# A decoder layer with sixteen experts: eight buffers for target rows, one softmax moved to the second expert, one power moved ahead of four sends

## The chip, the core and the metric

The kernel runs on one core of a Trainium2 chip. A core has four engines for computing: TensorE (PE in the profile; PEld is its loading of weights), VectorE (DVE), ScalarE (ACT) and GpSimd (POOL). SyncE (SP) issues transfers, as do ScalarE and GpSimd. Each engine works through its own list of instructions strictly in order and waits where an instruction's inputs or its buffer are not ready. The metric is the device time of one execution in microseconds (us); the median of the runs is compared.

## What is computed

One decoder layer on 1,024 tokens (16 sequences of 64) of 256 features in fp32: self-attention of 16 heads, cross-attention on a compressed context, and a feed-forward layer with a shared expert and 16 routed experts, each after a layernorm without weights. Only the last part matters here:

```python
scores = softmax(xt @ Wg.T)                    # 16 experts
sg = scores.reshape(T, 4, 4)                   # four groups
gmask = two best groups by their maximum
topi = top_k(where(gmask, sg, -inf), 4)        # four experts for a token
weights = take_along_axis(scores, topi)
h = silu(xt @ W1[e].T) * (xt @ W3[e].T)        # each expert e
y = sum over the chosen e of weights * (h @ W2[e].T)
z = (silu(xt @ Ws1.T) * (xt @ Ws3.T)) @ Ws2.T  # shared expert
x = x + y + z
```

The choice needs only the order of the logits, so the kernel takes it from the logits, and computes the softmax, which gives the weights, apart.

## The kernel before

The tokens lie in eight tiles of 128, in two halves of four tiles. Matrices that need more precision than one pass gives are split into a rounded part and a rest: ScalarE casts the rounded part (`parts_of`, L111; line L112 in the profile) and VectorE subtracts it from the source (L113).

**Towards the experts.** The third layernorm of the second half (`layernorm_t(3, (1,), ...)`, L1183) computes mean and variance on VectorE (L165 to L169), the variance to the power of -1/2 on GpSimd (`rstd`, L172), and a shift on VectorE (L176); ScalarE and VectorE scale the rows (L194, L187), TensorE turns them (L208). Then `choose(1)` (L1185) finds each token's four experts and, for each choice, the row in a DRAM array `xd` where the token goes (`targets`, L818). `send` (L821) writes rows by indirect DMAs, which GpSimd issues (L826), four for each choice of a half. The order on GpSimd around the change was: two choices of the first half (eight sends), choice 2 of the first half (four sends, L1197, not before the shared expert's last subtraction), the power `rstd` of the second half, choice 3 of the first half (L1200), and all four choices of the second half (sixteen sends, L1201).

**The routed experts.** Fifteen experts (e0 to e14) work on 384 slots each; the sixteenth is computed densely. The loop at L1336 runs in stages: its turn e loads the inputs of expert e, computes the hidden layer of expert e-1 and the output of expert e-2.

- `expert_inputs` (L1234): SP loads the expert's slots from `xd` into `xr` (three buffers; a load waits for the sends of the choices that can reach it). TensorE turns them, ScalarE and VectorE split them into `xs`. VectorE then copies one column, which says where each row of the output goes, as integers into `to` (L1253). `to` has four buffers.
- `expert_weights` (L1223, `weight_parts` at L268): SP loads 640 KB into a raw tile (two buffers), ScalarE casts them (L270), VectorE and, from the fourth expert on, also GpSimd subtract (L275).
- `expert_hidden` (L1256): 18 matmuls of 384 columns, silu on ScalarE (L1266, L1269), products on VectorE (L1267, L1270), the split into `hp`.
- `send_outputs` (L1274): 15 matmuls into two PSUM tiles, which two copies on ScalarE and one on VectorE evict into `y` (L1282; two buffers), and three indirect DMAs on GpSimd (L1287), which send the rows of `y` to where `to` says. `to` and `y` come free when these transfers have landed.

**The weights of the choices.** `weights_of_choices(half)` (L853) computes the softmax over 16 logits and picks each choice's weight: 14 short instructions on VectorE (L859 to L881, with `choices`, L726, among them) and an exp on ScalarE (L862). ScalarE holds the tables of either exp or silu, so a table is loaded ahead of the exp and another ahead of the next silu. The first half's call is at L1175; the second half's at L1360, in turn 6 of the loop. The results are read after the loop, when `add_outputs` (L1310) adds the experts' outputs, and by `add_last` (L934).

A planner puts the instructions of each engine in order, by a modelled timeline; `tc.issue_after(ins)` keeps what is written under it from being issued before `ins`.

Of the kernel before, what the change touches and what calls it, by code (L numbers as in the profile page):

```python
# [27 lines left out]
U32 = mybir.dt.uint32  # L28
# [15 lines left out]
SLOTS = 384  # L44
# [27 lines left out]
def decoder_layer(ctx: ExitStack, tc: tile.TileContext, a: dict, out: bass.AP):  # L72
# [79 lines left out]
    variances, rstds, shifts, highs, lows = [], [], [], [], []  # L152
    norms, scaled, turned, silus, exps, softened = [], [], [], [], [], []
# [153 lines left out]
    with ExitStack() as attn:  # L307
# [513 lines left out]
        def send(half, choices=range(TOPK), waits=()):  # L821

            to = targets[half]
            for k in choices:
                for i in range(4):
                    sent = nc.gpsimd.indirect_dma_start(  # L826
                        out=xd[: TOPK * NT + (E - 1 - k) * SLOTS],
                        out_offset=bass.IndirectOffsetOnAxis(ap=to[:, k, i : i + 1], axis=0),
                        in_=rows[half][i // 2][:, i % 2, :],
                        in_offset=None,  # L830
                    ).ins
                    side_by_side(sent, sent_rows)
                    sent_for[k].append(sent)
                    behind(sent, waits)
# [18 lines left out]
        def weights_of_choices(half):  # L853


            shape = [128, 4, E]
            lg = logits[half]
            m = fs.tile([128, 4], F32, tag="r_m", name="r_m")
            nc.vector.tensor_reduce(m, lg, AX.X, ALU.max)  # L859
            p = fs.tile(shape, F32, tag=f"r_p{half}", name=f"r_p{half}")  # L860
            nc.vector.tensor_tensor(p, lg, m.unsqueeze(2).broadcast_to(shape), ALU.subtract)
            exps.append(nc.scalar.activation(p, p, AF.Exp).ins)  # L862
            s = fs.tile([128, 4], F32, tag="r_s", name="r_s")
            nc.vector.tensor_reduce(s, p, AX.X, ALU.add)
            nc.vector.reciprocal(s, s)
            nc.vector.tensor_tensor(p, p, s.unsqueeze(2).broadcast_to(shape), ALU.mult)
            sel = selected[half]
            last = fs.tile([128, 4], F32, tag=f"cl{half}", name=f"cl{half}")
            nc.vector.tensor_tensor(last, sel[:, :, E - 1], p[:, :, E - 1], ALU.mult)
            nth = fs.tile(shape, F32, tag="slot", name="nth_back")  # L870
            nc.vector.tensor_tensor(
                nth, places[half], sel[:, :, E - 1 :].broadcast_to(shape), ALU.add
            )
            ch = choices(nth, sel)
            kept = fs.tile(shape, F32, tag="slot", name="kept")
            nc.vector.scalar_tensor_tensor(kept, over[half], 0.5, p, ALU.is_lt, ALU.mult)
            nc.vector.tensor_tensor(
                ch, ch, kept.unsqueeze(1).broadcast_to([128, TOPK, 4, E]), ALU.mult
            )
            w = fs.tile([128, TOPK, 4], F32, tag=f"cw{half}", name=f"cw{half}")  # L880
            nc.vector.tensor_reduce(w, ch, AX.X, ALU.add)  # L881
            return w, last, p
# [57 lines left out]
        routed = []  # L940


        with (
# [169 lines left out]
            for n in range(len(units) + 2):  # L1113
# [62 lines left out]
                if n == 9:  # L1176
                    rows[1] = [
                        xw.tile([128, 3, 2, 2, DC], F32, tag="w_s", name="rows1")
                        .rearrange("p a b c d -> p (a b c d)")[:, : 2 * ROW]
                        .rearrange("p (a b) -> p a b", a=2)  # L1180
                        for _ in range(2)
                    ]
                    normed[1] = layernorm_t(3, (1,), token_rows(1))[0]  # L1183
                    high = highs[-1]
                    scored, placed, aimed = choose(1)  # L1185
                    sh = [
                        xb.tile([128, 2, 2, 4 * HQ], F32R, tag=f"w_q{m}", name=f"sh{m}")
                        .rearrange("p a b c -> p (a b c)")
                        for m in range(2)
                    ]  # L1190
                    hs = []
                    for k in range(3):
                        with after(*pn_turned[(0 if k else 1) :]):
                            up = shared_up(0, k, xa)
                            part = [t[:, k * 512 : (k + 1) * 512] for t in sh]
                            hs.append(shared_hidden(k, *up, xa, part))
                    send(0, (2,), [lows[-1]])  # L1197
                    with after(projected, scaled[-1]):
                        shared_output(0, hs)
                    send(0, (3,), [high])  # L1200
                    send(1)  # L1201
                    with after(high):
                        dense_ups = dense_up(0, turned[-1], scored, scored)
                    with after(aimed, scored):
                        ups = [shared_up(1, 0, xa)]
                    with after(aimed, placed):
                        ups.append(shared_up(1, 1, xa))
                        hs = [shared_hidden(k, *ups[k], xa) for k in range(2)]
                        ups.append(shared_up(1, 2, xa))
                        hs.append(shared_hidden(2, *ups[2], xa))  # L1210
                        h_p = dense_gated(*dense_ups)
                        shared_output(1, hs)
                        dense_out(h_p, 0, range(4), add_last)
# [3 lines left out]
    fx = ctx.enter_context(tc.tile_pool(name="fx", bufs=2, reuse_waits="tile"))  # L1217
# [5 lines left out]
    def expert_weights(src, down_lo=nc.gpsimd):  # L1223
        return weight_parts(
            src,
            fw.tile([128, W_COLS], F32, tag="w123", name="w123"),
            [
                fw.tile([128, W_COLS], F32R, tag=f"w123{n}", name=f"w123{n}", bufs=3)
                for n in range(2)
            ],  # L1230
            down_lo,
        )

    def expert_inputs(e):  # L1234

        t = fx.tile([128, SLOTS // 128, ROW], F32, tag="xr", name="xr", bufs=3)
        first = TOPK * NT + (E - 2 - e) * SLOTS
        load = nc.sync.dma_start(
            out=t, in_=xd[first : first + SLOTS].rearrange("(b p) d -> p b d", p=128)
        ).ins  # L1240
        for k in range(min(TOPK, e + 1)):
            behind(load, sent_for[k])
        to = fx.tile([128, SLOTS // 128], U32, tag="to", name="to", bufs=4)
        parts = [fx.tile([128, 2, SLOTS], F32R, tag=f"xs{n}", name=f"xs{n}") for n in range(2)]
        for c in range(2):
            ps = at_tile([128, 512])[:, :SLOTS]
            for b in range(SLOTS // 128):
                nc.tensor.transpose(
                    ps[:, b * 128 : (b + 1) * 128], t[:, b, c * 128 : (c + 1) * 128], ident
                )  # L1250
            lows.append(parts_of(ps, parts[0][:, c, :], parts[1][:, c, :]))
        with tc.issue_after(lows[-1]):
            nc.vector.tensor_copy(to, t[:, :, D + e])  # L1253
        return parts, to
# [81 lines left out]
    for e in range(E + 1):  # L1336
        if e in (1, 2):

            low = lows[-1]
            hs[e - 1] = expert_hidden(ws[e - 1], xs[e - 1][0], SLOTS)  # L1340
        if e < E - 1:
            low = lows[-1]
            with tc.issue_after(up_done[0] if e in (1, 2) else low):
                xs[e] = expert_inputs(e)
            if e >= 1:
                with tc.issue_after(low), tc.issue_after(silus[-1]):
                    ws[e] = expert_weights(a["W123"][e], nc.vector if e < 3 else nc.gpsimd)
        if 0 <= e - 1 < E - 1 and e > 2:
            hs[e - 1] = expert_hidden(ws[e - 1], xs[e - 1][0], SLOTS)
        if e - 2 >= 0:  # L1350
            if e == E:

                with tc.issue_after(gated[0]):
                    h_p = dense_hidden(w_last, 1, 0)
            last = send_outputs(e - 2, ws.pop(e - 2), hs.pop(e - 2), xs.pop(e - 2)[1])
            if e - 2 == E - TOPK - 2:
                short = slots_are_short()
            if e == 6:
                with tc.issue_after(gated[0]), tc.issue_after(silus[-1]):
                    routed.append(weights_of_choices(1))  # L1360
            k = e - 2 - (E - 1 - TOPK)
            if k >= 0:
                got[k] = load_outputs(k)
# [135 lines left out]
```

## Time and profile before

| | |
|---|---|
| runs | 593.65, 597.68, 601.36 us (median 597.68) |
| the profiled execution | 590.21 us, of which the span is 588.4 |
| granted TensorE clock, mean | 0.979 of full speed |
| busy, share of the span | PE 92%, PEld 76%, DVE 68%, ACT 47%, POOL 39% |
| indirect output sends (L1287) | 45, mean 1084 ns on GpSimd, 2.4 to 7.1 us to landing |
| expert weights (`w<-in_W`) | 15 loads of 640 KB, median 4.7 us to landing |
| power on GpSimd (L172) | 1062 ns |
| table load on ScalarE | 1.28 us |

Times are microseconds from the span's start. In the page's slices a digit is a tenth of busy time. In the timeline each line gives start, length, engine, source line, operation, output and inputs, and in brackets how long the engine stood idle before it and whose end released it; "issue" there means that the profile shows nothing it waited for. Releasers are inferred, so an engine named as releaser may stand for a transfer that ended just then.

### The profile page before, as it was taken

The page shows a single profiled execution, that of the slowest core. Times are in us where ns is not written, and L with a number is a line of the kernel's source. Part 1 is how long each engine was busy: PE and PEld are TensorE (multiplying, and loading weights), DVE is VectorE, ACT ScalarE, POOL GpSimd, SP SyncE. Part 2 cuts the span into 40 slices and gives each one's busy share as a digit, 9 for nine tenths or more (in the row PEclk, how much of TensorE's full clock was granted, in tenths as well). Part 3 has the DMA queues.
Part 4 walks back from the last instruction along what each step waited for, and adds up shares of the span by engine and source line. Part 5 has one row for each costly group of instructions (what it writes and reads, how often), then busy time and mean ns, then how long its engine had stood idle before and what let it go on. Part 6 is the DMA issues. An engine that isn't in the chain of part 4 may idle for free.

```text
span 588.4 us, 10571 instructions
## 1 busy us (share of the span) xinstructions
PE 540.4 (92%) x3999; PEld 444.3 (76%) x3999; DVE 401.0 (68%) x879; ACT 279.4 (47%) x524; POOL 230.1 (39%) x213
## 2 busy tenths in 40 slices
PE   5979999999999999999999999999989778889962
PEld 4868988989889885667777577685778678879861
DVE  5434546475365788868476586889758667889876
ACT  3655575575745522231432323252625366857551
POOL 4192010010000104534343444632554646768762
PEclk9988999999999999999999999999999999999995
DMA  8667041240400398673020000000512676666384
GB/s 241 168 194 212 17 144 64 80 137 23 130 1 1 89 293 244 171 214 91 1 60 11 8 1 1 0 29 1 184 65 67 220 234 225 219 215 219 107 274 158
DMA packets 56293, 70.82 MB, mean 120 GB/s; under 512 B 13872, under 2 KB 42768, under 8 KB 56240
## 3 DMA queue, kind: packets, MB, share of 16 engines
q1 hardware_dynamic: 51408, 58.71, 33.6%
q0 software_dynamic: 3696, 10.36, 4.6%
q10 hardware_dynamic: 1136, 1.05, 0.5%
q8 instruction: 32, 0.52, 0.4%
q14 instruction: 21, 0.17, 0.1%
HBM read 48.61 MB, written 21.86 MB: 120 GB/s over the span
## 4 chain that ended last, share of the span: by engine, by line
PE 71%; DVE 12%; DMA 6%; ACT 4%; issue 4%; POOL 2%; SPq 0%; DVEq 0%; ACTq 0%; POOLq 0%
PE mm L104 42%; PE mm L989 6%; PE av L583 5%; PE at L566 4%; DMA yd<-y,to 4%; PE at L335 3%; PE at L1012 2%; PE av L1025 2%; PE av L104 2%; PE mm L431 2%; ACT w L270 2%; DVE rt L968 1%; DVE w L275 1%; DMA w<-in_W 1%; DVE x L1317 1%
## 5 line engine op out<-in xcount | busy, mean ns | idle before, releaser
L974 POOL TENSOR_TENSOR roped<-rt,rt 128x512 f32<-128x512 f32 x48 | 62.6, 1327 | 82.8 <-DVE rt L968 80.5
L968 DVE TENSOR_TENSOR rt<-mm,rope_q 128x512 f32<-128x512 f32 x96 | 61.5, 684 | 23.7 <-PE mm L104 23.0
L104 PE MATMUL mm<-xn,w_q 128*128 128x512 f32 x288 | 74.1, 403 | 0.5 <-ACT xn L214 0.5
L104 PEld LDWEIGHTS mm<-xn,w_q 128*128 128x128 f32 x288 | 52.1, 188 | 14.3 <-issue 2.6
L104 PE MATMUL mm<-xs,w 128*128 128x384 f32 x270 | 54.5, 344 | 8.3 <-ACT w L270 3.2
L1287 POOL DMA_INDIRECT yd<-y,to x45 | 48.8, 1084 | 26.0 <-ACT y L1282 7.5
L104 PEld LDWEIGHTS mm<-xs,w 128*128 128x128 f32 x270 | 45.8, 188 | 11.5 <-ACT w L270 4.2
L319 ACT ACTIVATE p<-p 128x512 f32<-128x512 f32 x32 | 20.2, 630 | 67.2 <-DVE p L318 67.2
L514 POOL TENSOR_TENSOR wo<-code,scale 128x512 fp32r<-128x512 f32 x8 | 10.6, 1328 | 103.2 <-PE mm L104 94.4
L989 PE MATMUL mm<-roped,w_s 128*64 128x512 f32 x192 | 46.3, 601 | 0.0
L606 DVE TENSOR_TENSOR x<-mm,x 128x256 f32<-128x256 f32 x64 | 26.0, 419 | 28.6 <-PE mm L104 27.4
L104 PE MATMUL mm<-wo,o 128*128 128x256 f32 x256 | 39.6, 295 | 0.1
L104 PE MATMUL mm<-wv,xn 128*128 128x256 f32 x256 | 37.0, 297 | 2.4 <-ACT kT L551 2.4
L104 PE MATMUL av<-w,hp 128*128 128x256 f32 x225 | 35.1, 289 | 4.0 <-DVE y L1282 3.3
L316 DVE TENSOR_REDUCE sm_m<-at 128x8 f32<-128x512 f32 x32 | 21.7, 680 | 22.8 <-PE at L566 21.9
L104 PEld LDWEIGHTS mm<-wv,xn 128*128 128x128 f32 x256 | 33.4, 197 | 3.5 <-ACT kT L551 2.6
L104 PE MATMUL mm<-xn,wk 128*128 128x512 f32 x128 | 35.6, 409 | 0.0
L104 PE MATMUL mm<-xn,wq 128*128 128x512 f32 x128 | 34.7, 407 | 0.4 <-ACT xn L214 0.4
L104 PEld LDWEIGHTS av<-w,hp 128*128 128x128 f32 x225 | 30.5, 188 | 5.7 <-DVE y L1282 3.9
L583 PE MATMUL av<-pt,v 128*128 128x128 f32 x256 | 34.5, 277 | 0.0
L104 PEld LDWEIGHTS mm<-wo,o 128*128 128x128 f32 x256 | 32.9, 190 | 1.5 <-issue 0.4
L583 PEld LDWEIGHTS av<-pt,v 128*128 128x128 f32 x256 | 32.0, 191 | 1.2
(216 smaller groups left out, 1138.8 us busy)
## 6 DMA issues: line engine op xcount, KB each, us to landing
w<-in_W SPq DMA_DIRECT2D x15, 640.0 KB, 4.7
code<-in_codes SPq DMA_DIRECT2D x32, 256.0 KB, 3.3
scale<-in_scales SPq DMA_DIRECT2D x32, 256.0 KB, 4.8
xr<-xd SPq DMA_DIRECT2D x15, 408.0 KB, 4.8
xd<-zeros SPq DMA_DIRECT2D x8, 720.0 KB, 7.0
yd<-zeros SPq DMA_DIRECT2D x8, 512.0 KB, 6.9
got<-yd SPq DMA_DIRECT2D x16, 256.0 KB, 4.3
wq<-in_Wq SPq DMA_DIRECT2D x4, 512.0 KB, 3.5
```

The costliest lines, as they stand in the source:

```text
L104: m = nc.tensor.matmul(ps, lhsT=l, rhs=r, start=(n == 0), stop=(n == len(pairs) - 1))
L270: nc.scalar.copy(w[0], t)
L316: nc.vector.tensor_reduce(m, sc, AX.X, ALU.max)
L319: exps.append(nc.scalar.activation(p, p, AF.Exp, scale=scale).ins)
L335: last = nc.tensor.transpose(ps[:, 2 * n : 2 * n + 2, :].rearrange("p a q -> p (a q)"), pn[:, 2 * n : 2 * n + 2, :].rearrange("p a k -> p ...
L566: nc.tensor.matmul(sc[par * 64 : par * 64 + 64, 2 * g + pp, :], lhsT=qk[0][:, b * S : (b + 1) * S], rhs=qk[1][:, b * S : (b + 1) * S], sta ...
L583: nc.tensor.matmul(av[:, k * 128 : (k + 1) * 128], lhsT=v[:, i, k0 : k0 + HD], rhs=pt[:, i].rearrange("p a q -> p (a q)"), start=True, sto ...
L606: nc.vector.tensor_tensor(x[i], ps, x[i], ALU.add)
L968: nc.vector.tensor_tensor(mt, ps3, rope_table(t, 2 * ab + k), ALU.mult)
L974: nc.gpsimd.tensor_tensor(r.rearrange("p (b s) -> p b s", s=S), one, two, op)
L989: nc.tensor.matmul(ps[h // 2][(h % 2) * 64 : (h % 2) * 64 + 64], lhsT=w_s[:, t, blk, ab, :], rhs=roped[2 * t + ab], start=first[h], stop=l ...
L1287: sent = nc.gpsimd.indirect_dma_start(out=yd[: (E - 1) * SLOTS + min(TOPK, E - 1 - e) * NT], out_offset=bass.IndirectOffsetOnAxis(ap=to[:, ...
```

## The change

Three edits, independent of each other in the text of the program:

```diff
-                    send(0, (2,), [lows[-1]])
+                    with tc.issue_after(rstds[-1]):
+                        send(0, (2,), [lows[-1]])
...
-        to = fx.tile([128, SLOTS // 128], U32, tag="to", name="to", bufs=4)
+        to = fx.tile([128, SLOTS // 128], U32, tag="to", name="to", bufs=8)
...
+        if e == 1:
+            with tc.issue_after(gated[0]), tc.issue_after(silus[-1]):
+                routed.append(weights_of_choices(1))
         if 0 <= e - 1 < E - 1 and e > 2:
...
-            if e == 6:
-                with tc.issue_after(gated[0]), tc.issue_after(silus[-1]):
-                    routed.append(weights_of_choices(1))
```

The first keeps the four sends of choice 2 behind the power of the third layernorm's second half, so that the power comes ahead of them on GpSimd. The second gives the target rows `to` eight buffers in place of four, 12 bytes a partition each. The third takes the second half's softmax from turn 6 of the loop to turn 1, after expert 0's last product has been split. In the planned order the softmax then stands on VectorE between the splits of e0 and e1's products, and its exp on ScalarE ahead of e1's silu. From e8 on the planner also sets some neighbouring instructions differently: on ScalarE the weight cast of some experts comes behind a silu and a cast that it came before, of others ahead of them, and on GpSimd three sends of e5 stand together ahead of a subtraction that stood between them.

## The prediction

> **What bounds the kernel now.** I first read the page's forty slices of 14.7 us. The columns are equal slices of the span, the digits tenths of busy time.
>
> ```profile
> PE   5979999999999999999999999999989778889962
> ...
> DMA  8667041240400398673020000000512676666384
> ```
>
> TensorE is full almost everywhere until slice 31; from there to slice 38 (about 456 to 557 us) it falls to 7 and 8 while the DMA engines stand at 5 to 7. That is the loop over fifteen routed experts (e0 to e14), and all three edits act there or just ahead of it. I split it into stretches: TensorE was busy 30.4 of 33 us (424 to 457), 24.1 of 33 (457 to 490), 13.9 of 14.5 (490 to 504.5), 21.8 of 26 (504.5 to 530.5), 23.2 of 25 (530.5 to 555.5). So the loop is bound by TensorE in good stretches and by something else in two bad ones. The timeline says by what; columns: start, length, engine, instruction, and in brackets the idle time before it and who ended it. Ahead of the loop:
>
> ```profile
> 431.70 0.96 POOL L826 DMA_INDIRECT xd<-wkq,to  x1 [0.30 <-issue]
> 432.69 1.06 POOL L172 TENSOR_TENSOR ln_rstd<-ln_var,half_power 128x4 f32<-128x4 f32 x1
> 433.78 0.16 DVE L176 SCALAR_TENSOR_TENSOR ln_shift<-ln_mv,ln_rstd 128x4 f32<-128x4 f32 x1 [3.94 <-POOL ln_rstd L172]
> ...
> 434.63 1.15 PE L208 MATMUL av<-ident,rows 128*128 128x128 f32 x8 [2.37 <-ACT rows L194]
> ```
>
> The variance was ready at 429.84, but the power stood behind four sends; VectorE waited 3.94 us, TensorE 2.37. At e3 and e4:
>
> ```profile
> 479.04 1.26 ACT L270 CAST w<-w 128x1280 fp32r<-128x1280 f32 x1 [4.77 <-DMA w<-in_W]
> ...
> 482.59 0.98 POOL L1287 DMA_INDIRECT yd<-y,to  x1 [0.16 <-DVE to L1253]
> ...
> 488.91 0.17 DVE L1253 CAST to<-xr 128x3 uint32<-128x3 f32 x1 [3.13 <-DMA yd<-y,to]
> ...
> 489.96 0.86 PE L104 MATMUL av<-w,hp 128*128 128x256 f32 x5 [2.46 <-DVE y L1282]
> ```
>
> e3's weights come late, since their load is queued on SP behind row loads that wait for the last send. e0's third output send then leaves at 482.59 and lands at 488.7; e4's target copy needs that buffer, and the eviction that TensorE wants stands behind the copy. At e6 to e9:
>
> ```profile
> 505.21 1.28 ACT L862 ACT_TABLE_LOAD   x1
> ...
> 506.78 1.28 ACT L1269 ACT_TABLE_LOAD   x1
> ...
> 509.89 1.33 PE L104 MATMUL mm<-xs,w 128*128 128x384 f32 x6 [1.35 <-ACT w L270]
> ...
> 516.68 0.85 PE L104 MATMUL av<-w,hp 128*128 128x256 f32 x5 [0.84 <-DVE y L1282]
> ...
> 523.91 0.57 DVE L1253 CAST to<-xr 128x3 uint32<-128x3 f32 x1 [2.01 <-issue]
> ```
>
> The softmax holds up a weight cast and an eviction; the send behind it lands at 523.83, and e9's target copy follows at 523.91. I read that "issue" as the same buffer wait. TensorE then idles 1.34 us to 525.40.
>
> **What the Trainium skill says.** "ScalarE: Activation LUTs", What ACT_TABLE_LOAD costs: about 1.28 us a load, and a drain of about 1.38. The trace agrees on the first; 505.21 follows the activation ahead of it by 0.02 us, so I add no drain. "DMA: Bandwidth & Descriptors", Anatomy of one DMA: about 2.0 us are fixed, mostly the receipt of the write. The output sends land 2.4 to 7.1 us after issue here: the fixed part is the floor, load makes the rest. "Perfetto Trace Analysis", Optimization Strategy: gaps that recur on the engine that should be full can mean too few buffers. Here they come twice, not steadily.
>
> **The power ahead of four sends.** Nothing is added; on GpSimd one instruction passes four sends, which pass no other send. It can start at 429.9, after the variance, and ends at 431.0 instead of 433.75: VectorE gains 2.8. TensorE gains only its idle 2.37, since its matmuls ahead run to 432.26; from 437.5 to 457 it was busy 19.44 of 19.5, so it carries the gain on. Price: the four sends left at 427.9 to 431.7 and now leave from 431.0, 1.265 apart, ending at 436.1; the next four, which waited for the casts until 436.96, end at 441.2. The second half's sixteen started at 447.3 when their targets came; with targets 2.4 earlier they start at 444.9, so the delay has 3.7 us of cover. Without it each microsecond would reach the row loads on SP and e3's weights queued behind them. The sixteen set those loads (last send 467.70, e3's load issued 472.69), so these come 2.4 earlier too. **-2.4** (0 to -2.8).
>
> **Eight target buffers.** The copies of e4 on no longer wait for sends four experts back. At e4 VectorE gains 3.13, and TensorE its 2.46, as the eviction follows directly. SP's row load for e7, held until that copy (489.1), also goes earlier; no TensorE wait on row loads shows after 472, so I price that at nothing. Late next: the y tile has two buffers, and e2's first eviction needs the same landing. It ran at 490.65, 1.9 us after the landing. Without the copy's wait it is ready some 5.5 us sooner, while the landing moves only by the 2.4 above, so ScalarE waits about 1 us for it; the row casts behind it are wanted by TensorE only some 4 us later, and hide that. **-2.5** (0 if y takes over, to -3.1).
>
> **The softmax taken to e1.** The same 14 VectorE instructions and two table loads, no transfer. VectorE: 0.22+0.21+0.22+0.63 ahead of e1's gating, 0.21+0.18 once exp is done, the rest (0.22, 0.16 or 1.26, 0.21, 0.41, 0.40) around and behind it: 3.1 in all, 4.2 as recorded at e6. ScalarE gets 1.28+0.26+1.28 = 2.82 between e0's last cast (466.5) and e1's silu (469.68), where it idled 3.14. But exp waits for VectorE, free at 468.75: exp at 469.7 (all times as before the shift), second table until 471.3, silu 1.6 late, and with VectorE's remaining rows 1.6 to 2.0. Behind it queue e2's weight cast and row casts, e0's evictions, and on SP e4's weight load, which waits for e2's raw tile and was cast 11 us after its issue. After these, ScalarE idled 4.77 and VectorE 3.94 for e3's weights; that wait is the cover. TensorE idled 1.57 there, so of 2.0 late 0.4 is left. Without that cover the whole delay stays. **+0.4** (0, as nothing is taken away there, to +3.5, the rows exposed).
>
> **The softmax gone from e6.** TensorE's idle 1.35, 0.84 and 0.34 (517.87) go, and with eight buffers 1.34 at e9: 3.9. From e7 to e10 the first matmuls took 509.89 to 530.53, 20.6 us for three; e10 to e14 took 24.9 for four, 6.2 each, so 18.6 would do, a gain of 2.0; plus 1.3 ahead of e7. I take **-3.3** (-1 to -3.9). From e8 some weight casts move behind two other ScalarE casts, others ahead; TensorE's waits on these casts were 0.3 to 1.4, 3.2 in all. Either sign: -2 to +2; I take 0. What follows e14 (555.5 to 588.4) starts from its last sends and is only moved.
>
> Sum: -2.4 - 2.5 + 0.4 - 3.3 = **-7.8** on the profiled execution's 590.21 (span 588.4 and 1.8 around it): 582.4. The median is 597.68, 7.5 longer; the trace cannot show where. The loop is where transfers end waits, so a longer execution probably lengthens waits that go away: I choose a quarter of the excess, 1.9. 597.7 - 7.8 - 1.9 = **588.0 us**.
>
> **The rivals.** *Longer waits in ordinary runs.* If most of the 7.5 sits in the target waits and e3's late loads, the gain is 7.8 and 5 to 7.5: 585 to 582, and 579 with the bounds above. For it: landings spread from 2.4 to 7.1; against it: matmul clock alone may make it. *The two y buffers take the waits over.* The same sends free both tiles; ScalarE did wait 0.50 at 524.01 for y. Then more target buffers only change the name of the wait, -2.5 goes, and half of -3.3: 594. *Landings grow in a denser loop, slower.* From e4 on, each y is refilled when the third send of two experts before has landed, and its own third send left 3.9 to 5.2, say 4.6, after the first eviction (y at 543.65, send at 547.58). So two experts take at least 4.6 plus a landing. At 6.2 an expert that allows 7.8; the longest landing was 7.1, the middle one 4.3. Pressing the same bytes into less time (0.72 of the DMA engines at 241 GB/s in the best stretch) could raise it. At 10 us an expert takes 7.3, eleven experts lose 12.1, and the sum is +4.3: **602**. It decides from 9.2, where the loss is 7.8. Against: no landing of 9 shows.
>
> **How the numbers follow.** Forecast 0.52 (its own range 584 to 592), longer waits 0.27, y 0.14, slower 0.07. Two per cent, about what a measurement of this kernel can tell from no change, is 12 us: under 585.7 or over 609.6. Of the forecast's share 0.12 falls under the former; with the first rival's 0.27 that gives faster 0.39. Slower by that much gets 0.04, half the last rival; the remaining 0.57 is within. The range 579 to 596 leaves about a tenth on either side.
>
> **What would show it.** Right: VectorE's 3.94 before the shift and TensorE's 2.37 gone; no wait of a target copy on an output send; tables loaded near 464 and 468, none after 500; e0 to e14 about 5 us shorter. Wrong: ScalarE waits on sends ahead of y of over 2 us each; e3's weights cast later than 478; e8 to e14 over 6.3 us each.

## The result, and the profile after

The changed kernel took **586.11 us** (median of 20 runs, 581.60 to 595.90) beside 597.85 us of the kernel before (20 runs, 589.96 to 603.32). The ratio is 0.9842, with a 95% interval of 0.9808 to 0.9876: a gain of under 2 per cent, but a clear one. It leaves out slow executions, such as five of the changed kernel's 20 that were over 1.5% above its fastest, and so isn't the ratio of these medians (0.980). The prediction was 588.0 us, within its range of 579 to 596. The profiled execution took 584.82 us, with a span of 583.1 (before: 590.21 and 588.4).

The slices of its page, 14.6 us each:

```profile
PE   5979999999999998999999999999999769999971
...
PEclk9998999999999999999999999999999899999995
DMA  8667041230500298755010000000411658777385
```

From slice 33 to 37 (481 to 554 us, counted from 0) TensorE is full, where it stood at 8 in three slices and at 9 in two before. Slices 31 and 32, where the loop starts, are as bad as they were, and PEclk, the granted clock, drops there. First the power, in the timeline of the changed kernel:

```profile
430.84 1.05 POOL L172 TENSOR_TENSOR ln_rstd<-ln_var,half_power 128x4 f32<-128x4 f32 x1 [7.55 <-DVE ln_var L169]
431.92 0.17 DVE L176 SCALAR_TENSOR_TENSOR ln_shift<-ln_mv,ln_rstd 128x4 f32<-128x4 f32 x1 [1.17 <-POOL ln_rstd L172]
432.09 1.04 POOL L826 DMA_INDIRECT xd<-wq,to  x1 [0.20 <-issue]
...
432.78 1.15 PE L208 MATMUL av<-ident,rows 128*128 128x128 f32 x8
```

The power now follows the variance and the four sends follow the power. VectorE waits 1.17 us where it waited 3.94; TensorE's line has no bracket, so its 2.37 are gone. Next, all that TensorE waited for between 482 and 555 us. In this view a line gives the waiting instruction, whose end released it, us in total, times, and the longest. The kernel before:

```profile
PE av L104 <- DVE y L1282: 3.3, 2, 2.5
PE mm L104 <- ACT w L270: 2.8, 4, 1.4
PE mm L104 <- DVE w L275: 2.0, 3, 1.3
PE av L104 <- DVE most L841: 0.5, 1, 0.5
```

The changed kernel:

```profile
PE mm L104 <- ACT w L270: 0.8, 2, 0.4
PE mm L104 <- issue: 0.6, 2, 0.4
PE at L1249 <- DVE xs L113: 0.2, 1, 0.2
```

8.6 us of waits became 1.6. Nor does VectorE or ScalarE stand idle ahead of a target copy, or ahead of an eviction into `y` other than for TensorE, in this stretch. But this execution gave some of it away at the start of the loop. The columns here are the stretch, its length, TensorE's busy time, the granted clock, the share of the DMA engines, and GB/s:

```profile
455.00:462.00 7.00, 3.30 (x27) 0.91 0.63 184
462.00:470.00 8.00, 6.39 (x24) 0.65 0.70 246
```

In 455 to 470 the kernel before had TensorE busy 12.1 of 15 us at full clock. Here it was busy 9.7, in part at 0.65 of the clock, so that e0's 18 matmuls took 5.73 us (3.85 before), and there were pauses that no instruction in the profile accounts for (1.67 us up to 458.57 is put down to "issue"). e0 began 3.5 us later than before, not 2.4 earlier. One profile can't tell whether the change brings this along; a repetition can. This profile also holds no landing of any transfer (its page leaves the times to landing out), and so do the four of the second session below. In these five the releasers are less sure, and "issue" can stand for a transfer: TensorE's 1.03 us ahead of e1's transposes are "issue" in the second profile of the whole change, where the kernel before has 0.98 us and the row load.

### The profile page after: what moved, and what is told of

It is laid out like the page before. It is cut to its first block, busy times and chain, and to the rows that moved or that the text cites. A ratio compares the mean times of both kernels' runs of the same rounds, so it can differ in the third digit from the quotient of the medians.

```text
span 583.1 us, 10571 instructions
## 1 busy us (share of the span) xinstructions
PE 541.0 (93%) x3999; PEld 446.5 (77%) x3999; DVE 401.6 (69%) x879; ACT 278.9 (48%) x524; POOL 230.4 (40%) x213
## 4 chain that ended last, share of the span: by engine, by line
PE 74%; DVE 10%; DMA 5%; ACT 3%; issue 3%; another core or an unknown queue 2%; SPq 1%; POOL 0%; DVEq 0%; ACTq 0%; POOLq 0%
PE mm L104 42%; PE mm L989 6%; PE av L104 5%; PE av L583 5%; PE at L566 3%; DMA scale<-in_scales 3%; PE at L335 3%; PE at L1012 2%; PE av L1025 2%; PE mm L431 2%; DMA code<-in_codes 1%; PE at L1249 1%; DVE rt L968 1%; PE mm L453 1%
## 5 line engine op out<-in xcount | busy, mean ns | idle before, releaser
L104 PEld LDWEIGHTS mm<-xs,w 128*128 128x128 f32 x270 | 48.0, 197 | 9.9 <-issue 3.7
L316 DVE TENSOR_REDUCE sm_m<-at 128x8 f32<-128x512 f32 x32 | 21.7, 679 | 23.6 <-PE at L566 22.6
L104 PEld LDWEIGHTS av<-w,hp 128*128 128x128 f32 x225 | 30.3, 189 | 2.3 <-issue 1.0
```

The source lines that it names most:

```text
L104: m = nc.tensor.matmul(ps, lhsT=l, rhs=r, start=(n == 0), stop=(n == len(pairs) - 1))
L316: nc.vector.tensor_reduce(m, sc, AX.X, ALU.max)
```

## The experiments

Theory A: three separate stalls of TensorE went, and each edit is worth its own. Theory B: the gain comes from something else that came along (at first the planner's new order from e8 on; later, that the start of the loop eats the power's gain). Theory C: rivals in which a gain is replaced or overlaps (the `y` buffers take the waits over, the softmax isn't covered at e1, the gains are the same gain). The runs were taken in three sessions of four kernels, each with its own runs of the kernel before: median 588.73, 592.92 and 588.38 us. The first two sessions were on one chip, the third on another. A gain in us below is worked out from the ratio to the kernel before, which is not quite the ratio of the medians; where medians are compared, it says so.

To compare traces I read intervals between expert silus (starts of the first silu of e0, e2, e6 and e14 in the timelines of ScalarE), in us:

| kernel | ratio to before | 95% interval | e0 to e2 | e2 to e6 | e0 to e6 | e6 to e14 |
|---|---|---|---|---|---|---|
| before | 1 | | 18.4 | 23.8 | 42.1 | 54.5 |
| power alone | 0.9930 | 0.9897–0.9962 | 18.3 | 23.3 | 41.7 | 54.5 |
| eight buffers alone | 0.9905 | 0.9876–0.9934 | 16.5 | 21.4 | 37.9 | 52.4 |
| softmax moved alone | 0.9910 | 0.9885–0.9934 | 17.2 | 24.5 | 41.8 | 48.7 |
| eight and softmax | 0.9842 | 0.9799–0.9885 | 16.6 | 20.7 | 37.3 | 48.4 |
| the same, again | 0.9848 | 0.9796–0.9901 | 17.5 | 20.9 | 38.4 | 48.4 |
| whole change | 0.9797 | 0.9749–0.9846 | 16.3 | 21.2 | 37.5 | 48.3 |
| without the eight | 0.9850 | 0.9812–0.9889 | 16.7 | 23.3 | 40.0 | 49.3 |
| without the softmax's move | 0.9859 | 0.9818–0.9899 | 18.3 | 21.0 | 39.3 | 52.4 |
| no second softmax | 0.9781 | 0.9732–0.9830 | 16.5 | 21.1 | 37.6 | 48.4 |
| softmax in turn 4 | 0.9826 | 0.9781–0.9872 | 17.6 | 24.0 | 41.6 | 48.4 |
| five buffers | 0.9796 | 0.9751–0.9841 | 16.5 | 20.8 | 37.3 | 48.4 |
| early weights | 0.9808 | 0.9767–0.9849 | 18.4 | 19.1 | 37.5 | 49.8 |

From e0 to e6 and from e6 to e14 TensorE runs the same number of matmuls in every kernel (early weights: two fewer, two more). At e2's silu it doesn't: in the whole change five matmuls, some 0.8 us by their lengths, stand behind it that stood ahead of it before. Each row is one profile, and a stretch at half clock (last section) adds up to 1.7 us to some of them, as to e2 to e6 with the softmax moved alone.

### Each edit alone

The power alone is the first hunk of the diff, the buffers alone and the softmax alone the other two, applied to the kernel before.

```diff
+                    with tc.issue_after(rstds[-1]):
+                        send(0, (2,), [lows[-1]])
```

> Only the power ahead of the four sends; buffers and softmax as before. Theory A (the three waits of the prediction, each worth what it was priced at): 2.4 us faster than before, ratio 0.996; VectorE's wait of 3.9 us ahead of the shift shrinks to about 1.1, TensorE's 2.4 us ahead of turning the rows is gone. Theory B (the gain is the planner's new order of the experts from e8 on): ratio 1.000 unless the order of the loop changes here too. Theory C (the sends held back cost what the power wins): ratio 1.000 and the first row load of the loop not earlier.

585.66 us (12 runs), against 588.73. Its intervals are about those of the kernel before, so the loop only starts earlier. TensorE's 2.4 us ahead of the transposes are gone from its trace. The gain by the ratio, 4.1 us, reaches from 2.2 to 6.1 and holds the 2.4.

```diff
-        to = fx.tile([128, SLOTS // 128], U32, tag="to", name="to", bufs=4)
+        to = fx.tile([128, SLOTS // 128], U32, tag="to", name="to", bufs=8)
```

> Only eight buffers for the targets. The order on TensorE, ScalarE, GpSimd and SP is then the one of before. Theory A: the waits of target copies on output sends are gone, 2.5 us at e4 and 1.3 at e9, ratio 0.994 to 0.996. Theory B: no gain, ratio 0.999 to 1.001, since the order is unchanged. Theory C (the two y buffers wait for the same sends): ratio 1.000 and ScalarE waiting over 1 us on output sends ahead of evictions.

583.72 us (11 runs): 5.6 us gained, where 2.4 to 3.5 were expected. The order of the instructions on TensorE, ScalarE, GpSimd and SP is that of the kernel before, and only one copy on VectorE stands elsewhere, so for this edit Theory B falls. Of Theory C a trace is there, as the timeline shows:

```profile
487.73 0.37 ACT L1282 COPY y<-av 128x256 f32<-128x256 f32 x1 [1.51 <-DMA yd<-y,to]
```

The eviction into `y` does wait for the same landing, 1.5 us. It costs TensorE nothing: e2 to e6 is 2.4 us shorter, close to the 2.46 that TensorE idled at e4. The gain beyond the expected shows from e0 to e2, ahead of any target copy that waited; there ScalarE's wait for e3's weights is 2.76 us, not 4.77. That it belongs to this edit isn't shown: with the power and the eight buffers together it is 4.52, and e0 to e6 is 2.4 shorter than with the power alone.

```diff
+        if e == 1:
+            with tc.issue_after(gated[0]), tc.issue_after(silus[-1]):
+                routed.append(weights_of_choices(1))
...
-            if e == 6:
-                with tc.issue_after(gated[0]), tc.issue_after(silus[-1]):
-                    routed.append(weights_of_choices(1))
```

> Only the softmax taken to turn 1, four target buffers, power where it was. Theory A: plus 0.4 at e1, minus 1.5 to 2.0 at e6 to e8, ratio 0.997 to 0.999. Theory B: the new order alone brings most of the 11.7 us, ratio 0.985 to 0.990. Theory C (the second expert's idle time covers nothing): ratio 1.000 to 1.003.

584.32 us (22 runs), 5.3 us gained, against 0.6 to 1.8 expected. In the trace e6 to e14 is 5.8 us shorter with the old four buffers, and TensorE waits on weight casts and their subtractions only 1.2 us after 482, where it waited 4.8. The ratio, 0.991, is nearer to Theory B's 0.985 to 0.990 than to Theory A's, and the edit brings the planner's new order along. How much of the gain is that order's is worked out below, in the part on the mis-sized terms.

> Eight buffers and the softmax in turn 1, the power where it was: the changed kernel without its first edit. Theory A: 0.9842 of before plus the power's 2.4 us, ratio 0.988. Theory B: 0.984 to 0.990, and no better than the softmax alone. Theory C: if the sum of single edits is less than this pair gives, one wait hid behind another; then this ratio is below the product of the two single ratios by over 0.003.

579.84 us (6 runs), 9.3 us gained; both edits alone sum to 10.9. They overlap between e6 and e14, which the buffers alone shorten by 2.1, the softmax alone by 5.8, and both by 6.1. By the first matmuls of the experts the overlap lies from e7 to e10: 20.6 us before, 18.6 with the buffers, 17.4 with the softmax moved, and 17.4 with both.

### Does the power still count on top?

> The whole change, beside the pair of eight buffers and the moved softmax, in one comparison. Theory A (the power ahead of the sends moves everything behind it by its 2.4 to 2.7 us, whatever the other two edits do): 0.980 of the time before, 2.4 to 2.7 us under the pair. Theory B (the pause of all engines near 442 and 456 and the granted clock of 0.5 at 462 in the profile of the changed kernel come with the earlier loop and eat the gain): 0.984 to 0.985, level with the pair, and its profile shows such a stretch near the loop's start again. If A holds, the profile shows none or shows it elsewhere.

> Eight target buffers and the moved softmax without the power edit, as the other side of that comparison. Both theories: 0.983 to 0.986 of the time before; TensorE between 482 and 555 waits 1 to 2 us in all, where the kernel before waited 8.6.

579.54 us for the whole change, 583.43 for the pair (6 runs each), 0.9797 against 0.9848: Theory A's numbers. The intervals overlap, and the pair's runs had the lower clock (mean 0.970 against 0.977), so the size stays rough. The whole change's second profile, with a span of 575.9, has no drop of the clock between 60 and 550 us; the pair's, without the power edit, has three, at 434, 462 and 479. So the disturbed start isn't the power's doing. TensorE's waits from 482 to 555, whole change (the first profile of the pair, which holds landings, has four such waits, 1.3 us, and puts all of them down to the cast):

```profile
PE mm L104 <- issue: 1.0, 3, 0.4
PE mm L104 <- ACT w L270: 0.4, 1, 0.4
```

### What the softmax costs at e1, and elsewhere

```diff
         if e == 1:
-            with tc.issue_after(gated[0]), tc.issue_after(silus[-1]):
-                routed.append(weights_of_choices(1))
+            routed.append(routed[0])
```

> The whole change without the second half's softmax: it is left out, and the first half's weights stand in for the second half's. What it still costs at e1. Theory A (the wait for e3's weights hides it but for 0.4 us): 0.001 under the whole change at most, so 0.979 to 0.980. Theory C (it costs its whole delay of 1.2 to 2.0 us at the start of the loop, where TensorE isn't full): 0.003 under the whole change, 0.976 to 0.977.

580.23 us (6 runs), against 579.54 with the softmax; by the ratios it is 0.0016 lower, between what the two theories expected and far within the intervals, so the times don't decide. The traces are sharper. From e0's silu to e1's it takes 7.1 us without the softmax and 8.3 with it, but to e6's, with the same matmuls between, 37.6 and 37.5. The delay of 1.2 us is there and is gone a few experts later: ScalarE has to wait for e3's weights in either case, 2.96 us without the softmax and 1.14 with it. That speaks for Theory A.

```diff
-        if e == 1:
+        if e == 4:
```

> The whole change with the second half's softmax in turn 4 of the loop, behind e2's last split, in place of turn 1. Theory A (from e4 on nothing hides it, since TensorE runs full there, as in turn 6 before): 2 to 3.5 us over the whole change, 0.984 to 0.986 of the time before, and TensorE's waits between 482 and 555 rise by 2 us or more. Theory C (what counts is that it is gone from e6 to e9, where it met the late sends; any earlier turn is as good): within 0.5 us of the whole change.

582.25 us (6 runs), 2.7 us over the whole change by the medians, but only 1.7 by the ratio: 0.9826, just under what Theory A expected, and the intervals overlap. The timeline shows what happens:

```profile
485.02 1.28 ACT L862 ACT_TABLE_LOAD   x1
...
487.74 1.28 ACT L1270 ACT_TABLE_LOAD   x1
...
487.77 1.31 PE L104 MATMUL mm<-xs,w 128*128 128x384 f32 x6 [0.58 <-ACT w L270]
...
497.36 2.35 PE L104 MATMUL mm<-xs,w 128*128 128x384 f32 x12 [1.55 <-DVE w L275]
```

The tables and a weight cast stand one after the other on ScalarE, TensorE waits for the cast, and for the next expert's subtraction on VectorE. Its waits from 482 to 555 sum to 4.1 us, 2.7 more than with the softmax at e1, as Theory A said, and e0 to e6 takes 41.6 us, not 37.5. By the traces the place matters, and e1 is good because a wait is there already.

### Each edit left out

> The whole change with four target buffers, the power and the moved softmax kept. Theory A (each edit takes away waits of TensorE that the others don't): the wait at e4 comes back, TensorE waits some 2.5 us on an eviction between 482 and 555, and the start of the loop loses up to 2 us more; 2.5 to 4.5 us over the whole change, which measured 0.980 of the time before, so 0.984 to 0.987. Theory C (the gains overlap; with the softmax gone from e6 the loop is full whatever the buffers): within 1 us of the whole change.

580.74 us (6 runs), 0.9850, with four target buffers. The wait at e4 is back, from the target copy to TensorE:

```profile
485.56 0.17 DVE L1254 CAST to<-xr 128x3 uint32<-128x3 f32 x1 [2.69 <-DMA yd<-y,to]
486.14 0.41 DVE L1283 COPY y<-av 128x256 f32<-128x256 f32 x1
...
486.61 0.86 PE L104 MATMUL av<-w,hp 128*128 128x256 f32 x5 [1.26 <-DVE y L1283]
```

The copy stands ahead of an eviction on VectorE, and TensorE waits for that. e2 to e6 takes 23.3 us again, 2.2 more, of which 1.3 is this wait; the trace doesn't put the rest down to one line.

> The whole change with the second half's softmax left in turn 6, the power and the eight buffers kept. Theory A: TensorE's waits on e7 to e9's weights, on their evictions and on the last subtractions come back, 4 to 5 us between 482 and 555, against 1.2 us less between e0's and e1's silu, which comes back later; 3 to 4.5 us over the whole change, 0.985 to 0.988 of the time before. Theory C (overlap): under 1.5 us over the whole change.

580.95 us (6 runs), 0.9859. e6 to e14 takes 52.4 us, as with eight buffers alone, and TensorE's waits from 482 to 555 sum to 4.8 us, 3.4 more than in the whole change. The softmax's old place in its timeline:

```profile
500.82 1.28 ACT L862 ACT_TABLE_LOAD   x1
...
502.39 1.28 ACT L1270 ACT_TABLE_LOAD   x1
...
505.50 1.31 PE L104 MATMUL mm<-xs,w 128*128 128x384 f32 x6 [1.36 <-ACT w L270]
...
512.29 0.86 PE L104 MATMUL av<-w,hp 128*128 128x256 f32 x5 [0.83 <-DVE y L1283]
```

The whole change has 0.9797, but from another session and the other chip. Against it, leaving out the eight costs 3.1 us and leaving out the move 3.6, at 588.4 us. Against the five buffers below, which have the whole change's order and were taken in the same session, it is 3.2 and 3.7. With the power's 3.0 (from the pair) this is about 9.7 of the whole 11.9. That the rest is what two edits share fits the overlap above; the intervals are too wide to show it by themselves.

### How many buffers, and is there a better kernel?

```diff
-        to = fx.tile([128, SLOTS // 128], U32, tag="to", name="to", bufs=8)
+        to = fx.tile([128, SLOTS // 128], U32, tag="to", name="to", bufs=5)
```

> The whole change with five target buffers in place of eight; the order on all engines is the same. Theory A (what held VectorE up was one send four experts back, issued 5 to 6 us ahead of the copy; five experts back it was issued 10 us ahead, and no landing took that long): the same as the whole change within 0.002, and no target copy waits. Theory D (the depth matters, since landings grow in the denser loop): 1 to 3 us over the whole change, with a target copy that waits on a send.

575.50 us (6 runs), ratio 0.9796: the same as eight (on the other chip), with no copy that waits on a send. The wait reached back four experts and not five. Two evictions into `y` waited 0.7 us each for a send, and one of these reached TensorE: with the targets free, `y` is the next to bind, though by little.

```diff
+            if e == 2:
+                with tc.issue_after(low), tc.issue_after(silus[-1]):
+                    ws[2] = expert_weights(a["W123"][2], nc.vector)
+                raw3 = fw.tile([128, W_COLS], F32, tag="w123", name="w123")
+                early = nc.sync.dma_start(out=raw3, in_=a["W123"][3]).ins
...
+                if e == 2:
+                    first.enter_context(tc.issue_after(early))
                 xs[e] = expert_inputs(e)
```

> A candidate: the whole change with e3's weight load issued on SP ahead of the row loads that wait for the last send of the tokens, some 5 us earlier. The planner then sets the loop differently from e2 on. Theory A (TensorE's idle time that is left lies between 457 and 482, and ScalarE's wait for e3's weights of 1.1 to 2.0 us is part of it): up to 1.5 us under the whole change, 0.977 to 0.980. Theory E (the load takes transfer time from e2's row load, which TensorE waits for as well, and the wait changes its name): 0.980 to 0.984.

577.47 us (6 runs), 0.9808: no gain, as Theory E said. TensorE's waits from 457 to 482:

```profile
PE at L1250 <- DMA xr<-xd: 3.4, 2, 2.8
PE mm L104 <- ACT xs L112: 0.8, 1, 0.8
```

The row load behind the early weights makes TensorE wait 2.8 us at once (the longest with five buffers was 1.3). The wait changed its name: e0 to e6 takes 37.5 us, as in the whole change. That e0 to e2 is long here and e2 to e6 short says little, since in this order 12 more output matmuls stand ahead of e2's silu. No version beat the whole change by more than its interval.

## Why the prediction was right, and which term was mis-sized

**The power, -2.4: right.** TensorE's 2.37 us went in every trace with this edit, and the loop's intervals didn't change (18.3, 23.3, 54.5). The four sends' delay had its cover, and the gain reached the loop: from the end of the variance to e0's first matmul it took 29.1 us before and 26.4 to 26.6 in the five profiles with the edit of the first and third sessions. In the second session all of it was slower by some 2 us or more, with the edit (28.7 to 29.2) and without (32.3).

**The target copy at e4, -2.5: right.** e2 to e6 shortened by 2.4 with the buffers alone, by 2.6 in the whole change, and grew by 2.2 when they were left out. The `y` tile took over waits of up to 1.5 us on ScalarE in five traces, as the prediction's "about 1 us", and all that reached TensorE was 0.7 us with five buffers. That rival had 594 us and is refuted. (Its sum leaves out the 1.9 that the forecast takes off; with it, it is 592.)

**The softmax at e1, +0.4 for its cover: right in mechanism.** 1.2 us late at e1, nothing at e6. The tables were loaded at 471.57 and 474.57 in the first profile, since its loop started late. In it the cover was partly used up:

```profile
474.57 1.28 ACT L1267 ACT_TABLE_LOAD   x1
...
476.88 1.26 ACT L270 CAST w<-w 128x1280 fp32r<-128x1280 f32 x1
478.57 0.79 PE L104 MATMUL mm<-xs,w 128*128 128x384 f32 x3 [2.10 <-ACT xs L112]
...
480.40 1.26 ACT L270 CAST w<-w 128x1280 fp32r<-128x1280 f32 x1
```

The cast of e3's weights has no bracket here: they were there, and ScalarE was late. "e3's weights cast later than 478" came true for that reason, and in the second profile the cast is at 475.85.

**The softmax gone from e6, -3.3, and the cast order, 0: the mis-sized terms.** e6 to e14 shortened by 6.2 us (54.5 to 48.3), not 3.3. On the marks that the prediction used, the first matmuls of the experts, the terms are these:

| first matmuls | before | predicted | eight buffers alone | whole change |
|---|---|---|---|---|
| e6 to e7 | 7.3 | 6.0 | 7.3 | 5.7 |
| e7 to e10 | 20.6 | 18.6 | 18.6 | 17.4 |
| e10 to e14 | 24.9 | 24.9 | 24.9 | 23.6 |

The prediction took e10 to e14's pace of 6.2 us an expert for what the loop would do. That pace still had 1.7 us of TensorE's waits in it, for casts of weights and for VectorE. Its own stretch at this place, TensorE busy 23.2 of 25 us, gives 5.8 an expert; at that floor the three rows gain 6.4 us, and 6.1 were measured on these marks. So the floor should have been TensorE's busy time per expert and not the best stretch seen. (The prediction also read TensorE at 7 and 8 up to slice 38; slices 36 and 37 of that page, which hold this stretch, stand at 9.) e10 to e14 lies far behind the softmax's old place, and it takes 24.9 with the softmax in turn 6 and eight buffers. So its 1.3 us are the planner's new order; TensorE's waits there fell from 1.7 to 0.8. The order, which came along with the softmax's move, was worth about 1 us where the prediction had 0, and part of the 1.2 from e7 to e10 may be its too: it begins at e8. No experiment changed it by itself.

**From e0 to e2: missed.** 18.4 us became 16.3, and the prediction had +0.4. Some 0.8 of this is only matmuls that changed sides of e2's silu. For the rest, e3's weights, which ScalarE waits for ahead of e2's silu, were cast 6.1 to 6.4 us after their load's issue before, with the power alone and with the softmax left in turn 6. It was 4.3 to 4.8 in five profiles with the softmax at e1, where the next weight load was issued 2 to 3 us behind and not 1. That would fit two loads that share the DMA engines. But with the buffers alone it was 4.3 with the next load 1 us behind, and without the second softmax 6.4 with it 3 us behind. So the cause stays open.

**The quarter of the excess, -1.9: the number fitted, the reason didn't.** The medians differ by 11.7 us, the ratio gives 9.4, the prediction said 9.7. The rival of longer waits, and the quarter taken from it, held that a longer ordinary execution holds longer waits that go away. Then the gain should be largest where the kernel before is slowest. No run shows that: 0.9842 at 597.85 us, 0.9797 at 592.92, and 0.9796 with five buffers at 588.38 (the intervals overlap). The sum should have been larger with nothing added: in the second profile the loop is 10.8 us shorter between e0's and e14's silu, where the prediction's three terms had 5.4. So the sum was too small and an addition without ground made it up; that the total fits is partly luck. What it could not see in one trace is below, the half clock that may follow a stall.

**Slower by longer landings: refuted.** In the changed kernel's two profiles no target copy, and no eviction in the loop, stood waiting for anything but TensorE. They hold no landings, but the profile with five buffers holds 34 of 45 output sends: 2.4 to 7.2 us, median 4.5, where the kernel before had 2.4 to 7.1 and 4.3. Landings do go with load: before, the eight slowest sends (5.6 us or more) had the DMA engines 0.72 to 0.96 busy in the 4 us after their issue, the eight fastest (under 2.9) 0.15 to 0.7. But the denser loop added little. e8 to e14's first matmuls took 35.3 us, 5.9 an expert, where 6.3 would have spoken against the forecast.

## What to carry to other kernels

When stalls are taken out of a loop whose bound is one engine, price the loop down to that engine's own busy time per turn; the best stretch seen still has waits in it, and a stall of TensorE can cost a stretch at half clock besides. A delay costs nothing where the delayed engine would have waited for something else soon after: look for the wait that ends later and put the work there. And a tile that a late transfer frees needs just enough buffers to reach past the landing: here five did what eight did.

## What was not expected of the hardware

**A stall can be paid twice.** With the buffers alone (no power edit) TensorE idles for 2.39 us behind the late power, and from 434.89 to 438.30 its clock is halved: six matmuls that took 1.65 us before take 2.81. Between 60 and 550 us the fourteen profiles have ten such stretches. Eight last 3.41 us, so that each costs up to 1.7; two last 6.83.

The Trainium skill, "TensorE: Matmul & The Clock Gate", The HAM clock gate, says that the clock is halved after an idle window of some 3.4 us, and that the windows run freely and don't restart with the kernel. Length, halving and free phase agree: within each of the fourteen profiles all changes of the clock lie on a grid of 3.413 us. But the window needn't be idle throughout. I summed TensorE's idle time in each window of this grid. Of some 2,000 windows at full clock, none with under 1.49 us of idle time was followed by half clock, two of twelve with 1.49 to 1.84 were, and all eight with 1.95 or more. So, as far as these profiles show, the place in the grid decides whether a stall is paid twice. Here is TensorE around the power's stall, first in the kernel before, then with eight buffers alone; the columns are the stretch, its length, TensorE's busy time, the granted clock, the share of the DMA engines, and GB/s:

```profile
430.09:433.50 3.41, 2.17 (x19) 1.00 0.31 115
433.50:436.92 3.42, 2.29 (x14) 1.00 0.03 10
```

```profile
431.48:434.89 3.41, 1.02 (x9) 1.00 0.14 50
434.89:438.30 3.41, 3.41 (x14) 0.50 0.13 43
```

In the first the stall falls on both sides of a window's end, 1.24 and 1.13 us, and the clock stays; in the second it lies in one window. With the softmax moved alone two stalls lie in one window each, the power's and the target copy's at e4 (busy 1.03 and 1.06 of 3.41 us), and half clock follows both. Behind the power's stall it came in three of the five profiles without the edit, and in none of the nine with it. By that share the stall costs 2.4 + 0.6 x 1.7 = 3.4 us on average, beside 4.1 measured alone and 3.0 on top of the pair. From the end of the variance to e0's first matmul the profiles without the edit took 30.3 and 30.4 us with half clock behind the stall, 29.1 and 29.2 without (the second session left out). This is read from fourteen profiles, with idle times that rest on modelled ends of matmuls; no experiment moved a stall within its window.

**Times and the clock.** In the 20 runs of the changed kernel time and mean clock go together, from 582.4 and 582.7 us at 0.975 to 595.9 at 0.961, about 0.8 us for 0.001 by a straight line. In the 38 runs of the kernel before in the first session it is 0.4. One stretch of 3.41 us at half clock takes 0.003 from the mean clock and costs up to 1.7 us, some 0.6 for 0.001. So the clock can't be all of it in the 20 runs, and what is cause and what is effect isn't shown.

**A slower session.** In the second session the kernel before took 592.9 us instead of 588.7 and 588.4, and from the variance to e0's first matmul all four of its profiles took some 2 us or more longer than their like in the other sessions. The first profile after is of this kind (31.7 us), with pauses of several engines at once: VectorE stood idle 2.01 us until 443.59, TensorE 1.67 until 458.57. They are also the five profiles without landings. What makes the pauses was not found.
